# Tap weights in 64x64 quarters of the TensorE array, with regrouped products, in a two-layer convolution and local-attention kernel

## The chip, the cores and the metric

The kernel runs on one core of a Trainium2 chip, as one launch. The metric is the device time in microseconds. A core has five engines with a queue of instructions each: TensorE (PE), VectorE (DVE), ScalarE (ACT), GpSimd (POOL) and SyncE (SP, which here only starts DMAs). All data are float32.

## The reference, cut to what matters

Eight images of 256 channels and 64x64 pixels pass through two layers, each `x = x + layer(group_norm(x))`.

```python
# layer 0: an involution-like convolution, REL=32, OUT=256, SHARE=8, 3x3
x1, x2, x3 = conv1x1(x, w1), conv1x1(x, w2), conv1x1(x, w3)       # 32, 32, 256 channels
h = relu(bn(concat([x1, unfold3(reflect_pad(x2))])))              # 320 channels
h = relu(bn(conv1x1(h, cw1)))                                     # 32 channels: the inner map
w = conv1x1(h, cw2, cb2).reshape(B, 32, 9, H, W)                  # the tap weights
out = einsum("bgskhw,bgkhw->bgshw", unfold3(pad(x3)), w)          # 9 products, summed
# layer 1: local attention, 7x7, 4 heads, beside a dynamic depthwise convolution
att = softmax(q . (unfold7(k) + position)); out_att = att . unfold7(v)
wts = softmax(conv1x1(x, Wfc).reshape(B, 256, 9, H, W), axis=2)
out_conv = sum_k(depthwise3(relu(depthwise3(x, w1)), w2) * wts)   # depthwise kernels alike for all k
out = rate1 * out_att + rate2 * out_conv
```

What the change touches is layer 0: the inner map `h` of 32 channels, the tap weights `w` that one matrix per tap makes of it, and the products of each tap's weights with the shifted map `x3`.

## The kernel before, in words

**Blocks and steps.** A picture is cut into NB = 8 bands of R = 8 rows. The main loop runs over blocks `g`, one block being one band of one image in layer 1; layer 0 runs AHEAD = 12 blocks ahead of it, so that while layer 1 works at band `g`, layer 0 makes the bands `g + 10` to `g + 12`. For `g < 0` layer 0 is alone (the code says `alone`; here called the front). A block has STEPS = 8 steps `s`: two channel tiles `ct` of four steps `m` each.

**The order is written by hand.** The scheduler is off (`manual_schedule`): every engine runs its instructions in the order in which the program emits them. A step has six places, each ended by `advance()`; `after(n, f)` puts `f` off by `n` places. The functions `beside(g, s)` and `steer(g, s)` say what of layer 0, of the keys, queries and values, and of the loads is emitted in which step: lists `head`, `mid` and `end` are run at three places of a step.

**What a step does in layer 1.** In even steps TensorE makes the scores (`scores`, tile `sco`, 64x64 quarters of the array: two heads by two query tiles) for this step and the next. `masked` (VectorE) adds the mask and takes the maximum; `exponentials` (ScalarE, L772), a reciprocal of the sum `tot` (VectorE, L779) and `probabilities` (ScalarE, L781) make the softmax; one step later `transposed` (tile `ptp`, copied to `pt`) and `weighted_values` (tile `small`) use it, and `add_values` adds to the output `xr`. In each step two `branch_weights` (tile `pf`, L886) go through ScalarE's `ex` (L891), which POOL sums (L1106). The depthwise convolution is 32 taps of VectorE per block (`acc`, L843 and L869), taken from a list `todo`: two in the second place of a step, and in the fourth place two in even steps and the rest in odd ones. At a tile's end `depthwise_end` has ScalarE write `oc` (L879), two buffers; `dynamic_sum` has POOL make `tot` (L899, L902), VectorE its reciprocal `rec` (L907), and POOL multiply and add into `xr` (L908, L912, L913). `keys` makes `pk` on TensorE, which VectorE turns into `kb` (L714, L721): for the next block in step 7 and for the second channel tile in step 3, in the first and last band in step 6 and 2. `first_stats` takes group-norm statistics (L287) of a later image.

**What a block does in layer 0.** `small_maps` (x1 and x2; ScalarE writes them, L347 and L351) in steps 0 and 1; `value_maps` (x3: tile `p`, L375, written by ScalarE as `x3n`, L380) emitted at the end of step 0 and in step 1; `hidden_maps` with its parts `one` and `two` in steps 4 and 6 makes the inner map `h2n`. The band is held as four pieces of two rows: partition `32 q + c` holds channel `c` of piece `q`. `tap_weights` multiplies `h2n` (128 partitions, 2 x 66 columns) by `c2[:, k]`, a 128x128 matrix with four equal 32x32 blocks on its diagonal, into a PSUM tile `pw` (L470), and then emits the products (`prod`, L483: a sum of `pw` and bias times the shifted `x3q`, 8 channels of a group at once). POOL adds each product to `xg` (L491); in the front every third goes through TensorE instead (L504). After the last, `take` has VectorE take statistics (L519) and the band is stored (L529).

Two tuples set the order: `TAPS_AT` the steps at whose end each group of taps is multiplied, `PRODUCTS_AT` the places after which its products follow. In the front it is three groups of three taps; otherwise groups of 2, 2, 2, 2 and 1 at the ends of steps 1 to 5.

**Buffers.** PSUM tiles with the tag `gen` (`pf`, `ptp`, `pw`, `p`, `pk`, `pq`, `pv`) share four buffers: a tile takes the one that came free first in the program's order, and its first matmul waits for the last reader of the tile that was there. `sco` has one buffer, products two (tag `prod`), `ex` three.

Of the kernel before, what the change touches and what calls it, by code (L numbers as in the profile page):

```python
# [18 lines left out]
P = 128  # L19
C = 256  # L20
# [16 lines left out]
SHARE = C // REL  # L37
PIECE = SR * W
RUN = (SR - 1) * (W + 2) + W
TG = 2, 3  # L40
HP = W + 2
HR = R + 2

# [20 lines left out]
STEPS = NCT * NT // 2  # L64


TAPS_AT = (1, 2, 3, 4, 5), (0, 2, 4)
PRODUCTS_AT = ((1, 2),) * 5, ((7, 14, 10), (9, 17, 13), (12, 20, 16))


CB3, CBQ, CBK, CBP, CWP0, CWP1, CW1, CW2, CBV = 0, 1, 2, 3, 4, 5, 6, 15, 24
# [16 lines left out]
def conv_layers_kernel(ctx: ExitStack, tc: tile.TileContext, ins: dict, out: bass.AP):  # L88
# [33 lines left out]
    c1 = load("c1", [P, 3, REL])  # L122
    gq = load("gq", [P, P])
    gc = load("gc", [P, NCT, P])
    c2 = load("c2", [P, KK, P], now=False)
    wq = load("wq", [P, NCT, C], ins["wq"].rearrange("(t p) n -> p t n", p=P), now=False)
    wk = load("wk", [P, NCT, C], ins["wk"].rearrange("(t p) n -> p t n", p=P), now=False)
    wv = load("wv", [P, NCT, C], ins["wv"].rearrange("(t p) n -> p t n", p=P), now=False)
# [13 lines left out]
    for t in probs + x3n + h2n:  # L142
        nc.gpsimd.memset(t, 0.0)

    def inverse_root(v):
# [45 lines left out]
    def layer1_loads():  # L191


        last = w1.tile([P, NCT, 1, C], F32, tag="oc", name="last")
# [218 lines left out]
    def hidden_maps(b, i, alone):  # L413
# [26 lines left out]
        def relu(v):  # L440
            nc.scalar.activation(h2, v, AF.Relu, bias=bn2b, scale=bn2s)

        def one(home):
            ph = conv(home, 0, 2, 0, 1)
            after(1, lambda: hidden(2))
            after(2, lambda: nc.scalar.copy(h2, ph))

        def two(home):
            ph = conv(home, 2, 3, 2, 2)
            after(1, lambda: nc.vector.tensor_add(h2, ph, h2))  # L450
            after(3, lambda: relu(h2))

        hidden(0)
        after(3 if alone else 5, lambda: hidden(1))
        if alone:

            home = ps.tile([P, 4 * P], F32, tag="acc", name=f"ph_{b}_{i}")
            after(7, lambda: conv(home, 0, 2, 0, 2))
            after(8, lambda: hidden(2))
            after(12, lambda: after(4, lambda ph=conv(home, 2, 3, 0, 2): relu(ph)))  # L460
        return [two, one]

    def tap_weights(b, i, u, alone, at):


        im = images[b]
        first, n = TG[alone] * u, min(TG[alone], KK - TG[alone] * u)
        pw = ps.tile([P, n, SR * HP], F32, tag="gen", name=f"pw_{b}_{i}_{u}", bufs=4)
        for j in range(n):
            nc.tensor.matmul(  # L470
                pw[:, j], c2[:, first + j], h2n[i % 2].rearrange("p r c -> p (r c)"), start=True, stop=True
            )

        def product(j):
            k = first + j
            if alone and j == n - 1:
                prod = w1.tile([P, NCT, RP, W], F32, tag="yp", name=f"prod_{b}_{i}_{k}", bufs=3)
                prod = prod.rearrange("p t r c -> p (t r c)")[:, : SHARE * SR * HP]
                prod = prod.rearrange("p (s n) -> p s n", s=SHARE)
            else:  # L480
                prod = w0.tile([P, SHARE, SR * HP], F32, tag="prod", name=f"prod_{b}_{i}_{k}", bufs=2)
            at = k // 3 * HP + k % 3
            nc.vector.scalar_tensor_tensor(  # L483
                prod[:, :, :RUN], pw[:, j, :RUN].unsqueeze(1).to_broadcast([P, SHARE, RUN]),
                par[:, PCB2 + k : PCB2 + k + 1],
                im.x3q[i].rearrange("p s r c -> p s (r c)")[:, :, at : at + RUN], ALU.add, ALU.mult,
            )
# [24 lines left out]

        def take():
            x = im.xg[i]
            if i == 0:
                im.st1 = stat.tile([P, 2 * NB, 6], F32, tag="st1", name=f"st1_{b}")
            for t in range(2):
                v = x[:, t * SHARE // 2 : (t + 1) * SHARE // 2].rearrange("p s r c -> p (s r c)")
                nc.vector.bn_stats(im.st1[:, 2 * i + t, :], v)  # L519
            im.x1[i] = dram.tile([C, BAND], F32, tag="x1", name=f"x1_{b}_{i}")  # L520
            if alone:
                after(9, lambda: keep(nc.scalar))
            else:
                keep(nc.sync)

        def keep(queue):
            for q in range(NQR):
                v = im.xg[i][q * REL : (q + 1) * REL].rearrange("p s r c -> p s (r c)")
                queue.dma_start(out=pieces(im.x1[i], q), in_=v)  # L529

        for j in range(n):
            after(at[j], lambda j=j: product(j))
# [342 lines left out]

    def depthwise_end(b, i, ct, acc):

        oc = w1.tile([P, BAND], F32, tag="oc", name=f"oc_{b}_{i}_{ct}")
        nc.scalar.activation(oc, acc.rearrange("p r c -> p (r c)"), AF.Copy, scale=rate2)  # L879
        return oc  # L880

# [45 lines left out]
    def beside(g, s):  # L927
# [57 lines left out]
        if 0 <= g + AHEAD - 1 < B * NB and s == (2 if alone else 1):  # L985
            bh, ih = divmod(g + AHEAD - 1, NB)

            def hidden():
                parts = hidden_maps(bh, ih, alone)
                if not alone:  # L990
                    convs.extend(parts)

            end.append(hidden)
        if 0 <= g + AHEAD - 2 < B * NB and s in TAPS_AT[g < -1]:
            u = TAPS_AT[g < -1].index(s)
            end.append(
                lambda: tap_weights(*divmod(g + AHEAD - 2, NB), u, g < -1, PRODUCTS_AT[g < -1][u])
            )
        return head, mid, end

    def steer(g, s):
# [5 lines left out]
        if s == 2 and n % NB == 0 and 0 < n < B * NB:  # L1007
            scaled_weights(n // NB)
        if s == (3 if g < -1 else 7) and g + AHEAD0 < B * NB:
            first_stats(*divmod(g + AHEAD0, NB), n=40 if g < -1 else 9)  # L1010
        if s == 5 and 0 <= g + 1 < B * NB:
            bn, inx = divmod(g + 1, NB)
            xr = images[bn].xr[inx] = x_tile("xr", bn, inx)
# [10 lines left out]
    with tc.manual_schedule():  # L1024
# [21 lines left out]
        for g in range(-AHEAD, B * NB):  # L1046
            b, i = divmod(g, NB)
            for s in range(STEPS):
# [81 lines left out]
def _layout(inputs):  # L1130
# [29 lines left out]
    arr["par"] = par  # L1160

    c2 = a["a_cw2"].reshape(REL, KK, REL).transpose(2, 1, 0)
    arr["c2"] = np.zeros((P, KK, P), f)
    for q in range(NQR):
        arr["c2"][q * REL : (q + 1) * REL, :, q * REL : (q + 1) * REL] = c2

    chan = np.zeros((C, NCHAN), f)
    chan[:, CB3] = a["a_b3"]
# [43 lines left out]
```

## Time and profile before

| what | value |
|---|---|
| median of 3 runs | 3852.04 us (3850.59 to 3853.89) |
| the profiled execution's own time | 3854.63 us |
| its span, first to last instruction | 3852.8 us |
| mean granted TensorE clock | 0.994 |
| PE matmul busy | 3756.3 us, 97% |
| PE weight loads busy (beside the matmuls) | 2109.9 us, 55% |
| DVE busy | 3434.4 us, 89% |
| ACT busy | 2809.2 us, 73% |
| POOL busy | 3116.8 us, 81% |
| DMA, mean | 127 GB/s |

The profile lists instructions with the line of the program that made them, the tile written and those read (`prod<-pw,c_par,x3q`), and shapes as partitions x elements. A float32 matmul shows as two records of equal length; the 576 taps are 1152 records of `pw`. Records of TensorE overlap[...]: what an instruction costs TensorE's queue is the time from its start to the next one's start, not its length. In the timeline, equal instructions that follow each other are merged (`x4`), with the start of the first and the time to the end of the last; a bracket at the end gives the engine's idle time ahead of it and what ended that.

### The profile page before, as it was taken

The page shows a single profiled execution, that of the slowest core. Times are in us where ns is not written, and L with a number is a line of the kernel's source. Part 1 is how long each engine was busy: PE and PEld are TensorE (multiplying, and loading weights), DVE is VectorE, ACT ScalarE, POOL GpSimd, SP SyncE. Part 2 cuts the span into 40 slices and gives each one's busy share as a digit, 9 for nine tenths or more (in the row PEclk, how much of TensorE's full clock was granted, in tenths as well). Part 3 has the DMA queues.
Part 4 walks back from the last instruction along what each step waited for, and adds up shares of the span by engine and source line. Part 5 has one row for each costly group of instructions (what it writes and reads, how often), then busy time and mean ns, then how long its engine had stood idle before and what let it go on. Part 6 is the DMA issues. An engine that isn't in the chain of part 4 may idle for free.

```text
span 3852.8 us, 71646 instructions
## 1 busy us (share of the span) xinstructions
PE 3756.3 (97%) x24620; PEld 2109.9 (55%) x24620; DVE 3434.4 (89%) x7125; ACT 2809.2 (73%) x6770; POOL 3116.8 (81%) x2100
## 2 busy tenths in 40 slices
PE   6889999999999999999999999999999999999998
PEld 3445555555555555555555555555555555555554
DVE  6879999999999999899998999999999899978877
ACT  4457777777777777777777777777777777677776
POOL 4868888888897888888888888888888888855565
PEclk9999999999999999999999999999999999999999
DMA  8764544544444544544544544454544544232221
GB/s 247 210 177 128 142 118 129 151 126 118 133 135 131 145 123 115 148 135 127 136 116 142 142 125 120 126 149 125 136 115 117 138 119 114 74 97 78 79 67 37
DMA packets 438926, 490.14 MB, mean 127 GB/s; under 512 B 62016, under 2 KB 324256, under 8 KB 438304
## 3 DMA queue, kind: packets, MB, share of 16 engines
q1 hardware_dynamic: 421984, 469.79, 44.1%
q10 hardware_dynamic: 16576, 15.76, 1.3%
q8 instruction: 194, 3.18, 0.4%
q14 instruction: 172, 1.41, 0.1%
HBM read 343.76 MB, written 145.10 MB: 127 GB/s over the span
## 4 chain that ended last, share of the span: by engine, by line
PE 81%; POOL 10%; DVE 3%; DMA 2%; ACT 2%; issue 2%; SPq 1%; ACTq 0%; POOLq 0%; DVEq 0%
PE pf L886 39%; PE small L799 6%; PE ptp L787 6%; POOL xg L491 6%; PE pk L706 5%; PE pq L684 5%; PE sco L750 5%; PE p L375 5%; PE pv L601 5%; PE pw L470 2%; POOL ex L1106 2%; PE small L332 1%; DVE prod L483 1%; PE small L434 1%; DMA x<-x3n 1%
## 5 line engine op out<-in xcount | busy, mean ns | idle before, releaser
L886 PE MATMUL pf<-yp,c_wfc 128*128 128x512 f32 x4096 | 1916.8, 594 | 11.3 <-DVE prod L483 6.3
L491 POOL TENSOR_TENSOR xg<-xg,prod 128x1024 f32<-128x1024 f32 x549 | 1199.8, 2185 | 132.5 <-DVE prod L483 103.6
L886 PEld LDWEIGHTS pf<-yp,c_wfc 128*128 128x128 f32 x4096 | 739.6, 190 | 711.4 <-issue 654.7
L1106 POOL TENSOR_TENSOR ex<-ex,ex 128x1024 f32<-128x1024 f32 x384 | 908.8, 2367 | 68.5 <-ACT ex L891 65.0
L891 ACT ACTIVATE ex<-pf 128x512 f32<-128x512 f32 x1024 | 604.0, 590 | 347.9 <-PE pf L886 269.2
L843 DVE SCALAR_TENSOR_TENSOR acc<-yp,c_chan,acc 128x504 f32<-128x504 f32 (+3 forms) x1104 | 775.5, 702 | 63.2 <-ACT acc L834 42.8
L483 DVE SCALAR_TENSOR_TENSOR prod<-pw,c_par,x3q 128x1040 f32<-128x1040 f32 x576 | 732.7, 1294 | 107.9 <-PE pw L470 60.8
L869 DVE SCALAR_TENSOR_TENSOR acc<-hid,c_chan,acc 128x504 f32<-128x504 f32 (+3 forms) x1024 | 751.1, 733 | 18.1
L781 ACT ACTIVATE prob<-prob,tot 128x196 f32<-128x196 f32 x1024 | 412.9, 452 | 242.4 <-DVE tot L779 236.8
L772 ACT ACTIVATE prob<-prob,nmax 128x196 f32<-128x196 f32 x1024 | 458.2, 450 | 101.3 <-DVE nmax L764 101.2
L907 DVE RECIPROCAL rec<-tot 128x256 f32<-128x256 f32 x256 | 445.7, 1741 | 28.3 <-POOL tot L902 27.5
L789 ACT COPY pt<-ptp 112x512 f32<-112x512 f32 x511 | 295.9, 579 | 111.8 <-PE ptp L787 111.8
L764 DVE CUSTOM_DVE_ANT_0 prob<-sco,c_mask 128x196 f32<-128x196 f32 x1024 | 324.8, 355 | 31.0 <-PE sco L750 31.0
L787 PEld LDWEIGHTS ptp<-ident,prob 128*112 128x112 f32 x2044 | 227.3, 133 | 184.4 <-issue 132.7
L787 PE MATMUL ptp<-ident,prob 128*112 128x128 f32 x2044 | 319.5, 279 | 0.0
L908 POOL TENSOR_TENSOR tot<-tot,rec 128x256 f32<-128x256 f32 x254 | 185.8, 732 | 145.7 <-DVE rec L907 139.7
L799 PEld LDWEIGHTS small<-pt,vt 112*64 112x64 f32 x8144 | 258.6, 138 | 79.8 <-issue 60.5
L799 PE MATMUL small<-pt,vt 112*64 112x64 f32 x8144 | 294.2, 225 | 3.3 <-DMA vt<-vd 1.8
L601 PE MATMUL pv<-c_wv,yp 128*128 128x256 f32 x1056 | 253.5, 383 | 1.8 <-ACT yp L572 1.8
L902 POOL TENSOR_SCALAR tot<-tot 128x512 f32<-128x512 f32 x127 | 243.9, 1920 | 11.1
L470 PEld LDWEIGHTS pw<-h2n,c_c 128*128 128x128 f32 x1152 | 175.1, 191 | 139.9 <-issue 115.9
L375 PE MATMUL p<-xc,w3s 128*128 128x512 f32 x512 | 243.3, 598 | 0.0
(136 smaller groups left out, 4656.7 us busy)
## 6 DMA issues: line engine op xcount, KB each, us to landing
vt<-vd SPq DMA_DIRECT2D x512, 112.0 KB
x3q<-x SPq DMA_DIRECT2D x128, 264.0 KB
xc<-in_x SPq DMA_DIRECT2D x64, 512.0 KB
xg<-in_xg SPq DMA_DIRECT2D x64, 512.0 KB
yp<-x SPq DMA_DIRECT2D x128, 256.0 KB
xr<-x SPq DMA_DIRECT2D x64, 512.0 KB
out_x<-xr SPq DMA_DIRECT2D x64, 512.0 KB
xs<-in_x SPq DMA_DIRECT2D x57, 512.0 KB
```

The lines of the kernel that those rows point to most:

```text
L483: nc.vector.scalar_tensor_tensor(prod[:, :, :RUN], pw[:, j, :RUN].unsqueeze(1).to_broadcast([P, SHARE, RUN]), par[:, PCB2 + k : PCB2 + k + 1],
L491: nc.gpsimd.tensor_add(im.xg[i], im.xg[i], rows(prod))
L601: nc.tensor.matmul(pv[:, g], yp[:, kt, r : r + 2].rearrange("p r c -> p (r c)"), wv[:, kt], start=(kt == 0), stop=(kt == NCT - 1),)
L772: nc.scalar.activation(prob[:, h, :NKEY], prob[:, h, :NKEY], AF.Exp, bias=nmax[:, h : h + 1], scale=-1.0, accum_out=tot[:, h : h + 1],)
L787: nc.tensor.transpose(ptp[:, h, ch], prob[:, h, ch * CHUNK : (ch + 1) * CHUNK], ident)
L799: nc.tensor.matmul(po[half[h], :, t * TQ : (t + 1) * TQ], im.vt[i + ch, m][:n, t, (2 * ct + h) * HD : (2 * ct + h + 1) * HD], pt[:n, h, ch ...
L843: nc.vector.scalar_tensor_tensor(o, yp[:, ct, ra + dr : rb + dr, ca + dc : cb + dc], chan[:, ct, CW1 + k : CW1 + k + 1], o, ALU.mult, ALU.add,
L869: nc.vector.scalar_tensor_tensor(o, hid[:, ra + dr : rb + dr, ca + dc : cb + dc], chan[:, ct, CW2 + k : CW2 + k + 1], o, ALU.mult, ALU.add,)
L886: nc.tensor.matmul(pf, wfc[:, kt, 2 * m + j, ct * P : (ct + 1) * P], images[b].yp[i][:, kt, PAD : PAD + R], start=(kt == 0), stop=(kt == N ...
L891: nc.scalar.activation(ex[:, j].rearrange("p (r c) -> p r c", r=R), pf, AF.Exp)
L907: nc.vector.reciprocal(rec, v)
L1106: after(4, lambda ex=ex, exb=exb: nc.gpsimd.tensor_add(ex, ex, exb))
```

## The change

- `c2` becomes 128x64 per tap: each half of the partitions holds its own two 32x32 blocks. A tap is no longer one 128x128 matmul but two of 64x64 (two instructions each), which write the lower and the upper half of the PSUM tile.
- A second copy of the inner map, `h2s`, has its halves exchanged: ScalarE writes it with two activations of 64 partitions just ahead of the one that writes `h2n`. A row half of the array can so make both halves of a tap: one from `h2n`, one from `h2s`. One tap of a group runs in the lower rows, another in the upper ones, each into a tile of its own.
- Outside the front the taps form four groups, (0, 1 | 2), (3 | 4), (5 | 6), (7 | 8), at the ends of step 7 of the block before and of steps 1, 3 and 5, each just ahead of scores. In the front the groups stay, all in the lower rows, two quarters at a time.
- The products of the first group follow after 1, 2 and 3 places, of the others after 1 and 2. Products have three buffers instead of two.
- In even steps one depthwise tap instead of two is emitted in the fourth place; the odd step that follows takes it.
- `first_stats` takes its statistics after 15 places instead of 9 (outside the front); the last front block's inner map is written 4 places later.
- `oc` has one buffer instead of two, which makes room.

In the program as built, TensorE has two small matmuls for each of the 576 large ones, ScalarE 128 activations more, POOL one memset more; VectorE has as many instructions as before in another order; SP's queue is the same.

```diff
+HALF = P // 2
-TAPS_AT = (1, 2, 3, 4, 5), (0, 2, 4)
-PRODUCTS_AT = ((1, 2),) * 5, ((7, 14, 10), (9, 17, 13), (12, 20, 16))
+TAPS = (((0, 1), (2,)), ((3,), (4,)), ((5,), (6,)), ((7,), (8,))), tuple(((k, k + 1, k + 2), ()) for k in (0, 3, 6))
+TAPS_AT = (-1, 1, 3, 5), (0, 2, 4)
+PRODUCTS_AT = ((1, 2, 3), (1, 2), (1, 2), (1, 2)), ((7, 14, 10), (9, 17, 13), (12, 20, 16))
...
-    c2 = load("c2", [P, KK, P], now=False)
+    c2 = load("c2", [P, KK, HALF], now=False)
...
+    h2s = const.tile([P, SR, HP], F32, name="h2s")
...
         def relu(v):
+            for a, z in ((0, HALF), (HALF, 0)):
+                o, z = slice(a, a + HALF), slice(z, z + HALF)
+                nc.scalar.activation(h2s[o, :, :W], v[z], AF.Relu, bias=bn2b[z], scale=bn2s[z])
             nc.scalar.activation(h2, v, AF.Relu, bias=bn2b, scale=bn2s)
...
-            after(12, lambda: after(4, lambda ph=conv(home, 2, 3, 0, 2): relu(ph)))
+            after(12, lambda: after(gap, lambda ph=conv(home, 2, 3, 0, 2): relu(ph)))
...
-        first, n = TG[alone] * u, min(TG[alone], KK - TG[alone] * u)
-        pw = ps.tile([P, n, SR * HP], F32, tag="gen", name=f"pw_{b}_{i}_{u}", bufs=4)
-        for j in range(n):
-            nc.tensor.matmul(
-                pw[:, j], c2[:, first + j], h2n[i % 2].rearrange("p r c -> p (r c)"), start=True, stop=True
-            )
+        lots = TAPS[alone][u]
+        ks = [k for lot in lots for k in lot]
+        n = len(ks)
+        pws = [
+            ps.tile([P, len(lot), SR * HP], F32, tag="gen", name=f"pw_{b}_{i}_{u}_{r}", bufs=4)
+            for r, lot in enumerate(lots) if lot
+        ]
+        side = [slice(0, HALF), slice(HALF, P)]
+        for m in range(len(lots[0])):
+            for q in range(2):
+                for r, lot in enumerate(lots):
+                    if m < len(lot):
+                        h2 = (h2n[i % 2] if q == r else h2s)[side[r]].rearrange("p r c -> p (r c)")
+                        nc.tensor.matmul(pws[r][side[q], m], c2[side[r], lot[m]], h2, start=True, stop=True)
+        weights = [pw[:, m] for pw, lot in zip(pws, lots) for m in range(len(lot))]
...
-                prod = w0.tile([P, SHARE, SR * HP], F32, tag="prod", name=f"prod_{b}_{i}_{k}", bufs=2)
+                prod = w0.tile([P, SHARE, SR * HP], F32, tag="prod", name=f"prod_{b}_{i}_{k}", bufs=3)
...
-        oc = w1.tile([P, BAND], F32, tag="oc", name=f"oc_{b}_{i}_{ct}")
+        oc = w1.tile([P, BAND], F32, tag="oc", name=f"oc_{b}_{i}_{ct}", bufs=1)
...
-            first_stats(*divmod(g + AHEAD0, NB), n=40 if g < -1 else 9)
+            first_stats(*divmod(g + AHEAD0, NB), n=40 if g < -1 else 15)
...
-                    for _ in range(2 if m % 2 == 0 else len(todo)):
+                    for _ in range(1 if m % 2 == 0 else len(todo)):
                         todo.pop(0)()
```

More of the change, by code (lines that the diff above doesn't have):

```diff
@@ L39 @@
 RUN = (SR - 1) * (W + 2) + W
-TG = 2, 3
+HALF = P // 2
 HP = W + 2
@@ L141, in conv_layers_kernel @@
     h2n = [const.tile([P, SR, HP], F32, name=f"h2n_{i}") for i in range(2)]
-    for t in probs + x3n + h2n:
+    h2s = const.tile([P, SR, HP], F32, name="h2s")
+    for t in probs + x3n + h2n + [h2s]:
         nc.gpsimd.memset(t, 0.0)
@@ L191, in layer1_loads @@
     def layer1_loads():
-        last = w1.tile([P, NCT, 1, C], F32, tag="oc", name="last")
+        last = w1.tile([P, NCT, 1, C], F32, tag="oc", name="last", bufs=1)
         for f in late:
@@ L411, in x_by_group, with hidden_maps @@
         nc.sync.dma_start(out=t.rearrange("p s r c -> p (s r c)"), in_=ins["xg"][b, i])
-    def hidden_maps(b, i, alone):
+    def hidden_maps(b, i, alone, gap):
         im = images[b]
@@ L466, in tap_weights @@
         im = images[b]
-        first, n = TG[alone] * u, min(TG[alone], KK - TG[alone] * u)
-        pw = ps.tile([P, n, SR * HP], F32, tag="gen", name=f"pw_{b}_{i}_{u}", bufs=4)
-        for j in range(n):
-            nc.tensor.matmul(
-                pw[:, j], c2[:, first + j], h2n[i % 2].rearrange("p r c -> p (r c)"), start=True, stop=True
-            )
+        lots = TAPS[alone][u]
[13 more added lines that the diff above has]
+        weights = [pw[:, m] for pw, lot in zip(pws, lots) for m in range(len(lot))]
         def product(j):
-            k = first + j
+            k = ks[j]
             if alone and j == n - 1:
@@ L480, in product @@
             else:
-                prod = w0.tile([P, SHARE, SR * HP], F32, tag="prod", name=f"prod_{b}_{i}_{k}", bufs=2)
+                prod = w0.tile([P, SHARE, SR * HP], F32, tag="prod", name=f"prod_{b}_{i}_{k}", bufs=3)
             at = k // 3 * HP + k % 3
             nc.vector.scalar_tensor_tensor(
-                prod[:, :, :RUN], pw[:, j, :RUN].unsqueeze(1).to_broadcast([P, SHARE, RUN]),
+                prod[:, :, :RUN], weights[j][:, :RUN].unsqueeze(1).to_broadcast([P, SHARE, RUN]),
                 par[:, PCB2 + k : PCB2 + k + 1],
@@ L988, in hidden @@
             def hidden():
-                parts = hidden_maps(bh, ih, alone)
+                parts = hidden_maps(bh, ih, alone, 4 if g < -1 else 8)
                 if not alone:
@@ L993, in beside @@
             end.append(hidden)
[L994 to L998, printed above, removed]
+        for gt, st in ((g, s), (g + 1, s - STEPS)):
+            front = gt < -1
+            if 0 <= gt + AHEAD - 2 < B * NB and st in TAPS_AT[front]:
+                u = TAPS_AT[front].index(st)
+                end.append(
+                    lambda gt=gt, u=u, front=front: tap_weights(
+                        *divmod(gt + AHEAD - 2, NB), u, front, PRODUCTS_AT[front][u]
+                    )
+                )
         return head, mid, end
@@ L1162, in _layout @@
     c2 = a["a_cw2"].reshape(REL, KK, REL).transpose(2, 1, 0)
-    arr["c2"] = np.zeros((P, KK, P), f)
+    arr["c2"] = np.zeros((P, KK, HALF), f)
     for q in range(NQR):
-        arr["c2"][q * REL : (q + 1) * REL, :, q * REL : (q + 1) * REL] = c2
+        o = q * REL % HALF
+        arr["c2"][q * REL : (q + 1) * REL, :, o : o + REL] = c2
     chan = np.zeros((C, NCHAN), f)
```

## The prediction

> **What bounds the kernel now.** I read the page first, then five long windows of equal length, then one regular block (image 4, band 1, from 2146.70 us, with the end of the block before it) engine by engine in the timeline.
>
> ```profile
> PE 3756.3 (97%) x24620; PEld 2109.9 (55%) x24620; DVE 3434.4 (89%) x7125; ACT 2809.2 (73%) x6770; POOL 3116.8 (81%) x2100
> ```
> ```profile
> 2050.00:2500.00 450.00, 447.61 (x2980) 253.12 (x2979) 415.13 (x868) 338.28 (x820) 388.59 (x257) 1.00 0.48 132
> ```
>
> The columns of the second line are the window, its length, then busy time of PE, weight loads, DVE, ACT and POOL. TensorE is busy 99.5% of the stretch, VectorE 92%. So in the long middle part TensorE sets the pace and any instruction taken from its queue counts, as long as the other queues keep up; VectorE has 8% to spare and no more. A regular block is 56.9 us from its first scores to the next block's.
>
> The tap weights in TensorE's timeline:
>
> ```profile
> 2102.35 0.61 PE L470 MATMUL pw<-h2n,c_c 128*128 128x132 f32 x4
> 2102.90 0.92 PE L750 MATMUL sco<-kb,qb 64*64 64x196 f32 x16
> 2103.74 1.15 PE L799 MATMUL small<-pt,vt 112*64 112x64 f32 x32
> ...
> 2126.35 0.61 PE L470 MATMUL pw<-h2n,c_c 128*128 128x132 f32 x4
> 2126.80 1.88 PE L886 MATMUL pf<-yp,c_wfc 128*128 128x512 f32 x4
> ```
>
> From start to start, four instructions (two taps) take 0.45 ahead of pf and 0.55 ahead of scores: 0.22 a tap, and 0.10 for going over to the 64x64 tiles. Nine taps are 1.98 us of each block.
>
> The stretch from the keys of step 7 to the second value map, in the same block's TensorE, VectorE and ScalarE timelines:
>
> ```profile
> 2141.02 1.88 PE L706 MATMUL pk<-yp,c_wk 128*128 128x512 f32 x4
> ...
> 2146.70 0.92 PE L750 MATMUL sco<-kb,qb 64*64 64x196 f32 x16
> ...
> 2157.29 1.02 PE L375 MATMUL p<-xc,w3s 128*128 128x512 f32 x2
> ```
> ```profile
> 2143.47 1.28 DVE L519 BATCH_NORM_STATS2 st<-xg 128x6 f32<-128x512 f32 x2
> 2144.67 0.74 DVE L714 SCALAR_TENSOR_TENSOR kb<-pk,c_chan,pe 128x512 f32<-128x512 f32 x1
> 2145.32 0.53 DVE L721 SCALAR_TENSOR_TENSOR kb<-pk,c_chan,pe 128x16 f32<-128x16 f32 x3
> 2145.76 1.53 DVE L869 SCALAR_TENSOR_TENSOR acc<-hid,c_chan,acc 128x504 f32<-128x504 f32 x2
> 2147.20 0.16 DVE L779 RECIPROCAL tot<-tot 128x2 f32<-128x2 f32 x1
> ```
> ```profile
> 2152.46 0.80 ACT L781 ACTIVATE prob<-prob,tot 128x196 f32<-128x196 f32 x2
> 2153.16 1.40 ACT L347 ACTIVATE x<-small,bias 32x252 f32<-32x252 f32 x3
> 2154.57 0.47 ACT L351 ACTIVATE x<-small,bias 32x256 f32<-32x256 f32 x1
> 2155.06 0.60 ACT L891 ACTIVATE ex<-pf 128x512 f32<-128x512 f32 x1
> ```
>
> What to see: ScalarE runs these without a gap, and its ex ends at 2155.66, 1.63 us before the p at 2157.29. In the built program, before and after, that p waits for this ex, whose PSUM buffer it takes. Pk ends at 2142.90, but VectorE comes to kb only at 2144.67: it is 1.8 us late, and so never waits for pk. Both margins matter below.
>
> [...] sixteen score instructions, 196 columns each, take 0.85 us, where 196 columns of a full-width matmul are 0.164 (pf: 1.72 for 4x512), 2.6 us one after the other; and the change costs the 0.10 above.[...]
>
> **The change part by part, in a regular block.**
> *TensorE.* The scores make four rounds of four tiles in 0.75 (0.85 less 0.10 on leaving the mode), 0.187 a round against 0.164 of streaming. A round of 132 columns streams 0.111; with 0.01 to 0.025 on top, 0.12 to 0.135. One pair of taps is two rounds, 0.25; the group of three taps is four, 0.5. Sum 0.5 + 3 x 0.25 = 1.25 against 1.98: **0.73 saved**. All four groups stand ahead of scores, so the change of mode moves to the front of the group and is not added. Over 55 blocks this is 40 us, if nothing waits.
> *VectorE.* As many instructions as before, reordered. Products stood two at the turn into each of steps 2 to 5 and one at 6; now three stand at the turn into step 0 and two at each of 2, 4, 6. One conv tap per pair of steps goes from even to odd, first_stats (1.20) into step 1. This evens the load, and VectorE comes to step 6 without lag: from the turn into step 2 it has four products (4.9 us) less before it than now, where it takes up the last product at 2136.19, 3.0 us after its weights. It therefore comes early to kb in step 7 and must now **wait for pk**. Behind kb stand, in the program's order, up to the recip that releases ScalarE's prob: kb 1.09, two taps 1.44, BN stats 1.20, recip 0.12, three taps 2.17, product 1.22, masks 0.57, xr 0.52, product 1.22, two taps 1.44, product 1.22, recip 0.16. With 0.04 to start (a product began 0.04 after its pw ended) this is 12.4 us after pk. ScalarE then needs 0.04 + prob 0.70 + maps 1.90 + ex 0.60 = 3.2, and p 0.05 more: p can start **15.7 us after pk ends**. TensorE would be there after 14.39 (2157.29 - 2142.90) + 0.5 for the new group = 14.9. So p waits 0.8. The 1.63 of margin is used up, because prob starts 8.15 after the scores of step 0 where it started 5.76 after them.
> *Sum of a regular block:* -1.98 + 1.25 + 0.8 = +0.1. On top, p's weight load is no longer hidden (0 to 0.19), and the next ptp waits for x3n, which runs 5.9 after that ex where TensorE needs 5.7 (0 to 0.2). I take +0.2, with 0 to +0.5 as ends. The regular blocks with value maps ahead are bands 1 to 6: 39 of them, **+8 us**.
> *Band 7:* its keys are made in step 6, so VectorE does not wait in step 7; the recip is 1.3 earlier and the margin holds: 7 x -0.73 = -5. *Band 0:* keys in step 6 too, but the one-row depthwise piece puts a ScalarE round trip ahead of the products: between -0.73 and +0.3, I take 7 x -0.4 = -3. The last two blocks with taps have no value maps: -1.5.
> *ScalarE* gets 128 halves of the relu; a full one is 0.46 to 0.48 and the same columns are worked, so 0.4 each, 0.8 a block at step 6, where it stands idle about 1 us at a time (prob for tot, 1.04). Cost nothing; without that cover 0.8 a block.
> *POOL* does the same work (85% busy), xg adds filling its wait of 3.5 us for the x maps. Adds in step 2 need the buffer of the product three back, long done. *One oc buffer:* ScalarE's oc in step 4 must wait for POOL's xr; adding the adds of 2.2 and the other POOL rows, xr ends 14.8 after the scores of step 2 and oc comes at 15.7. Nothing, with 0.9 to spare. SP's queue keeps its order.
> *Front (first 250 us).* One row half only, two tiles at a time, so no tap gets faster; a change of mode each side, 0.1 to 0.2 per group, two groups of a block on its chain, eight blocks: +2 to +3. The third product buffer takes away up to the 6 us that products wait for POOL there, though the chain runs mostly through TensorE, ScalarE and DMA. I take +1, from -5 to +6. The smaller c_c2 load and h2s's memset: nothing, hidden by the input loads. The waits with 0 given could also gain: bound 0.1 a block.
>
> *All:* +8 - 5 - 3 - 1.5 + 1 = about 0. The profiled execution took 3854.6 us (span 3852.8), 2.6 above the median 3852.0; the sum stands against its own time, and moved to the median gives **3852**.
>
> **Rivals.**
> 1. *The gain stays.* VectorE, or the ScalarE queue, is faster than my chain and p does not wait: 3852 - 40 = 3812; with half of it, 3832. For it: TensorE at 99.5%. Against: every link of the 15.7 is a measured row.
> 2. *Slower: the oc buffer.* If POOL comes over 0.9 us later than worked out, ScalarE stands at oc at the turn of steps 3 and 4, with the acc of the next conv, pt and ex behind it, and VectorE's taps wait in turn. 0.6 a block beyond the point over 39 blocks: +23, 3875.
> 3. *The quarters don't overlap* in these small shapes: 36 instructions of 0.111 are 4.0 us instead of 1.98, +2 a block, 3960. The scores speak against it.
>
> **How the numbers follow.** The wait taking the gain back: 0.61, its own range 3838 to 3872 (regular blocks 0 to +0.5, band 0 and front to their ends). The gain stays: 0.20. The oc buffer or another second wait: 0.14. No overlap: 0.05. A measurement tells about 0.2%, 8 us, from no change; of the first case 0.13 lies faster, 0.32 within and 0.16 slower. Faster 0.33, same 0.32, slower 0.35. The range 3828 to 3882 leaves out the lower part of rival 1 and rival 3.
>
> **What would show it.** Right: pw groups of 0.25 and 0.5; VectorE idle at kb behind pk once a regular block; p waiting for ex by some 0.8, about 40 times, and blocks of 57.0 us. Band 7 shorter by 0.7. Wrong: no wait at p and blocks of 56.2; oc waiting for xr; or pw groups of 0.4 and more.

## The result and the profile after

The changed kernel took **3898.2 us** (median of 4 runs, 3893.4 to 3901.1), the kernel before 3851.7 beside it: ratio **1.0117**, 95% interval 1.0101 to 1.0133, so it is slower by about 46 us. The forecast was 3852, with 3828 to 3882 as range. The profiled execution took 3901.1 us, its span 3899.3.

The first part of the page after, and the window that was shown of before:

```profile
PE 3739.2 (96%) x25772; PEld 2038.1 (52%) x25772; DVE 3399.9 (87%) x7125; ACT 2868.5 (74%) x6898; POOL 3120.7 (80%) x2101
```
```profile
2050.00:2500.00 450.00, 436.44 (x3021) 238.16 (x3020) 401.53 (x848) 343.00 (x826) 378.83 (x256) 1.00 0.46 127
```

TensorE has 17 us less busy time in all and works 97% of the stretch where it was 99.5%: it stands still 13.6 us of 450, against 2.4. VectorE and POOL are less busy there than before, ScalarE by 4.7 us more, 76% in all. So no engine became the bound by its load; waits did.

What TensorE waits for, over the whole span (waited for: us in total, times, longest):

```profile
PE p L377 <- ACT ex L905: 43.9, 52, 1.8
PE ph L436 <- ACT hid L426: 22.1, 12, 4.0
PE small L813 <- ACT x L353: 21.3, 52, 0.4
PE pg_a L244 <- DVE mv_a L238: 20.8, 1, 20.8
PE pf L900 <- DVE prod L497: 10.0, 6, 1.7
```

The first and the third are new, with 65 us (small had waited once, 1.5 us); ph and pg_a lie in the front and were there before. The tap weights themselves, at the turn into image 4, band 2, and what follows them:

```profile
2237.75 0.32 PE L485 MATMUL pw<-h2n,c_c 64*64 64x132 f32 x1
...
2238.25 0.86 PE L764 MATMUL sco<-kb,qb 64*64 64x196 f32 x14
2239.04 1.15 PE L813 MATMUL small<-pt,vt 112*64 112x64 f32 x32
...
2249.59 1.98 PE L377 MATMUL p<-xc,w3s 128*128 128x512 f32 x4 [0.65 <-ACT ex L905]
...
2254.78 1.15 PE L813 MATMUL small<-pt,vt 112*64 112x64 f32 x32 [0.41 <-ACT x L353]
```

From the first pw to small it is 1.29; scores alone took 0.85, so three taps cost 0.44. The same for every place of this block, from start to start in us, in the kernel before, in the one after, and in the fastest kernel of the experiments (experiment 8, "final" here); places that did not change are left out:

| TensorE, image 4, band 2 | before | after | final |
|---|---|---|---|
| (taps and) scores of step 0 | 0.85 | 1.29 | 1.29 |
| ptp to the second p | 0.44 | 1.25 | 0.44 |
| that p | 1.72 | 1.82 | 1.72 |
| pf, (change of mode,) taps and scores of step 2 | 3.11 | 3.36 | 2.88 |
| pf and taps of step 3 | 2.17 | 1.72 | 1.72 |
| pf, taps and scores of step 4 | 3.12 | 2.89 | 2.89 |
| two pf and taps of step 5 | 3.88 | 3.43 | 3.43 |
| pf, taps and scores of step 6 | 2.89 | 2.88 | 2.89 |
| sum against before | | +0.5 | -0.9 |

VectorE and ScalarE between the keys of step 7 and those two waits, same block:

```profile
2233.99 0.75 DVE L728 SCALAR_TENSOR_TENSOR kb<-pk,c_chan,pe 128x512 f32<-128x512 f32 x1 [0.94 <-PE pk L720]
...
2239.99 1.30 DVE L497 SCALAR_TENSOR_TENSOR prod<-pw,c_par,x3q 128x1040 f32<-128x1040 f32 x1
...
2244.93 1.29 DVE L497 SCALAR_TENSOR_TENSOR prod<-pw,c_par,x3q 128x1040 f32<-128x1040 f32 x1
2246.14 0.15 DVE L793 RECIPROCAL tot<-tot 128x2 f32<-128x2 f32 x1
```
```profile
2246.33 0.81 ACT L795 ACTIVATE prob<-prob,tot 128x196 f32<-128x196 f32 x2 [2.28 <-DVE tot L793]
2247.05 1.40 ACT L349 ACTIVATE x<-small,bias 32x252 f32<-32x252 f32 x3
2248.45 0.47 ACT L353 ACTIVATE x<-small,bias 32x256 f32<-32x256 f32 x1
2248.95 0.60 ACT L905 ACTIVATE ex<-pf 128x512 f32<-128x512 f32 x1
2249.57 0.69 ACT L382 ACTIVATE x3n<-p,bias 128x512 f32<-128x512 f32 x1
...
2251.98 0.81 ACT L795 ACTIVATE prob<-prob,tot 128x196 f32<-128x196 f32 x2
2252.80 1.43 ACT L349 ACTIVATE x<-small,bias 32x252 f32<-32x252 f32 x3
2254.26 0.47 ACT L353 ACTIVATE x<-small,bias 32x256 f32<-32x256 f32 x1
```

VectorE stands at kb until pk ends (2233.95), and from there to the end of the reciprocal (2246.29) it does not pause: 12.3 us. ScalarE then works from prob at 2246.33 to the second half of the maps at 2254.73 without a pause either. Two waits hang on this one queue: ex releases p at 2249.59, and the maps' second half releases small at 2254.78, since `small` has one PSUM buffer and x1 and x2 lie in it. Ahead of that, ScalarE had stood 2.28 us at step 0's prob; in the old order it did not stand there at all (image 4, bands 1 to 7).

Not every band lost the same. From first scores to first scores, before and after (median of the same band over images 1 to 4), and the change summed over all images (4 and 5 together):

| band | 0 | 1 | 2 | 3 | 4, 5 | 6 | 7 |
|---|---|---|---|---|---|---|---|
| before | 58.1 | 56.9 | 56.9 | 59.6 | 56.9 | 56.5 | 60.8 |
| after | 59.8 | 57.7 | 57.3 | 60.4 | 57.3 | 56.7 | 63.9 |
| sum | +8.6 | +5.6 | +3.4 | +5.3 | +4.6 | +0.2 | +14.8 |

With +4.2 before the first scores these make the 46 us. Band 7 stands out. Its step 6 (image 3) in TensorE's timeline, and the granted clock there:

```profile
2102.71 0.62 PE L801 MATMUL ptp<-ident,prob 128*112 128x128 f32 x4
2105.00 3.65 PE L900 MATMUL pf<-yp,c_wfc 128*128 128x512 f32 x4 [1.67 <-DVE prod L497]
2108.47 2.55 PE L720 MATMUL pk<-yp,c_wk 128*128 128x512 f32 x8
```
```profile
2104.00:2105.00 1.00, 0.00 (x1) 0.03 (x1) 1.00 (x3) 0.84 (x4) 0.83 (x2) 1.00 1.14 190
2105.00:2107.00 2.00, 2.00 (x3) 0.97 (x4) 1.96 (x5) 0.00 (x0) 2.00 (x1) 0.52 1.13 202
2107.00:2109.00 2.00, 2.00 (x4) 0.73 (x4) 1.21 (x1) 0.25 (x1) 2.00 (x2) 0.63 1.09 329
2109.00:2112.00 3.00, 3.00 (x11) 1.71 (x10) 1.59 (x7) 2.51 (x6) 2.84 (x4) 1.00 0.82 227
```

(Window, length, busy time and instructions of PE, weight loads, DVE, ACT, POOL, then the granted clock.) The pf waits for the PSUM buffer that the product of tap 8 reads last. It starts 2.29 after ptp instead of the usual 0.49: 1.8 us late, where it was 1.2 late before. Then a pf that usually takes 1.72 takes 3.47, at a granted clock of 0.52 from 2105 to 2107. That happened in four of the six such places of this execution; at 1.7 us each it is some 7 of band 7's 14.8.

### The profile page after: what moved, and what is told of

Same layout as the page of the kernel before. It is cut to its first block, busy times and chain, and to the rows that moved or that the text cites. A ratio compares the mean times of both kernels' runs of the same rounds, so it can differ in the third digit from the quotient of the medians.

```text
span 3899.3 us, 73816 instructions
## 1 busy us (share of the span) xinstructions
PE 3739.2 (96%) x25772; PEld 2038.1 (52%) x25772; DVE 3399.9 (87%) x7125; ACT 2868.5 (74%) x6898; POOL 3120.7 (80%) x2101
## 4 chain that ended last, share of the span: by engine, by line
PE 70%; DVE 12%; ACT 8%; POOL 4%; issue 3%; DMA 2%; SPq 1%; ACTq 0%; POOLq 0%; DVEq 0%
PE pf L900 35%; PE small L813 6%; PE ptp L801 5%; PE pv L615 5%; PE pq L698 5%; PE pk L720 5%; DVE prod L497 4%; PE sco L764 3%; ACT x L349 2%; POOL xg L505 2%; PE p L377 2%; DVE acc L883 2%; PE pw L485 2%; DVE acc L857 2%; ACT prob L786 1%
## 5 line engine op out<-in xcount | busy, mean ns | idle before, releaser
L900 PEld LDWEIGHTS pf<-yp,c_wfc 128*128 128x128 f32 x4096 | 747.5, 191 | 741.4 <-issue 653.5
L857 DVE SCALAR_TENSOR_TENSOR acc<-yp,c_chan,acc 128x504 f32<-128x504 f32 (+3 forms) x1104 | 773.7, 701 | 55.9 <-ACT acc L848 35.5
L813 PEld LDWEIGHTS small<-pt,vt 112*64 112x64 f32 x8144 | 258.3, 138 | 104.7 <-issue 60.2
L377 PE MATMUL p<-xc,w3s 128*128 128x512 f32 x512 | 249.0, 610 | 43.9 <-ACT ex L905 43.9
L793 DVE RECIPROCAL tot<-tot 128x2 f32<-128x2 f32 x512 | 81.6, 159 | 198.4 <-ACT prob L786 197.4
```

The source lines that it names most:

```text
L813: nc.tensor.matmul(po[half[h], :, t * TQ : (t + 1) * TQ], im.vt[i + ch, m][:n, t, (2 * ct + h) * HD : (2 * ct + h + 1) * HD], pt[:n, h, ch ...
L857: nc.vector.scalar_tensor_tensor(o, yp[:, ct, ra + dr : rb + dr, ca + dc : cb + dc], chan[:, ct, CW1 + k : CW1 + k + 1], o, ALU.mult, ALU.add,
L900: nc.tensor.matmul(pf, wfc[:, kt, 2 * m + j, ct * P : (ct + 1) * P], images[b].yp[i][:, kt, PAD : PAD + R], start=(kt == 0), stop=(kt == N ...
```

## The experiments

**Theory:** the order of VectorE's queue. Three products stand between VectorE's restart at kb and step 0's reciprocal; ScalarE's queue, and p and small behind it, come too late. **Rival A:** the quarters themselves or the two half activations cost the time. **Rival B:** the single oc buffer.

**1. One product behind the reciprocal.**

```diff
-PRODUCTS_AT = ((1, 2, 3), (1, 2), (1, 2), (1, 2)), ((7, 14, 10), (9, 17, 13), (12, 20, 16))
+PRODUCTS_AT = ((1, 2, 4), (1, 2), (1, 2), (1, 2)), ((7, 14, 10), (9, 17, 13), (12, 20, 16))
```

> The changed kernel with the third product of the first group one place later, behind the reciprocal of step 0 instead of ahead of it. Theory (VectorE's order: three products ahead of step 0's reciprocal make ScalarE's prob, maps and ex late, TensorE then waits at p and, in step 2, at small): the chain from pk to p loses one product, 1.22 us, so the waits at p (0.8 in a regular block, 1.6 in band 0) and at small (0.4) go; regular block 57.3 to 56.1, total 3898 - 52 x 1.2 = about 3834, below the kernel before. Rival A (the quarters or the extra half activations themselves cost the time): within 5 us of 3898. Rival B (the one oc buffer): within 5 us of 3898.

Measured 3836.0, ratio to before 0.9954 (0.9937 to 0.9970). One number in one tuple turns 46 us lost into 18 gained. Regular blocks went from 57.3 to 56.1. TensorE's waits:

```profile
PE pf L900 <- DVE prod L497: 9.9, 6, 1.7
PE small L813 <- ACT x L353: 7.4, 18, 0.4
...
PE p L377 <- ACT ex L905: 3.1, 7, 0.5
```

Both new waits shrink together, 65 us to 10.5, though nothing near p or small was touched; quarters, half activations and oc buffer are those of the changed kernel. This settles for the theory, and against A and B as the main cause. In regular blocks about 0.2 stayed ahead of small, too short for the list of waits but plain from start to start (scores to small 1.00 in place of 0.80). The six waits at pf in band 7 are untouched, and the clock fell in four of them here too.

**2. The conv taps back.**

```diff
-                    for _ in range(1 if m % 2 == 0 else len(todo)):
+                    for _ in range(2 if m % 2 == 0 else len(todo)):
```

> The changed kernel with the conv taps back where they were: two in the second half of an even step instead of one. Theory: in step 7 the three taps between kb and the reciprocal become two, 0.72 us off the chain from pk to p, and step 6 gets 0.72 more, which VectorE's wait at kb (1.2 us on average) takes up: p waits 0.1 instead of 0.8 in a regular block and small hardly, about -1.0 a block, total about 3850. Rivals A (quarters) and B (oc buffer): no change, 3898; if the even load matters more, slower than 3898.

Measured 3865.0, 1.0029 (1.0021 to 1.0036): a gain of 33 us where 48 was expected. The p of a regular block starts 15.0 us after pk instead of 15.65, and the waits of p fall from 43.9 to 21.9 us in total. So the tap counts on the chain to p, as worked out. Small did not follow: 21.5 us in 52 waits, as in the changed kernel. The lines above say why. ScalarE's second maps end 5.2 us after the ex that releases p (2254.73 against 2249.55), and TensorE, once p has started, comes to small in 4.7 (p 1.82 and the 2.88 of the final column). As long as p starts right behind ex, small is late by the same amount, however late ex is.

**3. The diagonal quarters, in the changed order.**

```diff
-            for a, z in ((0, HALF), (HALF, 0)):
-                o, z = slice(a, a + HALF), slice(z, z + HALF)
-                nc.scalar.activation(h2s[o, :, :W], v[z], AF.Relu, bias=bn2b[z], scale=bn2s[z])
...
-                        h2 = (h2n[i % 2] if q == r else h2s)[side[r]].rearrange("p r c -> p (r c)")
-                        nc.tensor.matmul(pws[r][side[q], m], c2[side[r], lot[m]], h2, start=True, stop=True)
+                        h2 = h2n[i % 2][side[q]].rearrange("p r c -> p (r c)")
+                        nc.tensor.matmul(pws[r][side[q], m], c2[side[q], lot[m]], h2, start=True, stop=True)
```

> The changed kernel in its own order, but each tap from the two diagonal quarters of its own half of the map, one tap at a time, and no exchanged copy: TensorE needs as long per tap as before, ScalarE is rid of the half activations. Theory: TensorE gets 0.9 a block more, of which the first group's 0.44 lies ahead of the late p and only shortens its wait: +0.4 to +0.5 a block, about 3898 + 25 = 3922, so that the order by itself costs 70 us against the kernel before. Rival A (the half activations on ScalarE cost the time): 3870 or less.

Measured 3904.5, 1.0130 (1.0115 to 1.0145); expected about 3922. The p still starts 15.65 us after pk, to the hundredth: the half activations, absent here, have no part in that chain. Regular blocks went from 57.3 to 57.8, inside what was expected (0.4 to 0.5), as p and small wait less (29.8 and 10.5 us in all) when TensorE comes later. The rest of the miss is band 7, 1.9 shorter in most images: there the wait is for VectorE anyway, and after the slightly shorter idle the clock fell once in six places. With p late, 0.9 a block more of TensorE's work cost some 5 us in all: in a regular block half of it went where TensorE would have waited, in bands 0 and 1 more (0.2 is left), and band 7 came out shorter.

**4. Quarters at the old places.**

The kernel before with the quarters, the exchanged copy and half-width c2, and five groups of two taps, the last of one; outside the front all else is as it was (cut to the order):

```diff
+TAPS = (((0,), (1,)), ((2,), (3,)), ((4,), (5,)), ((6,), (7,)), ((8,), ())), tuple(((k, k + 1, k + 2), ()) for k in (0, 3, 6))
 TAPS_AT = (1, 2, 3, 4, 5), (0, 2, 4)
 PRODUCTS_AT = ((1, 2),) * 5, ((7, 14, 10), (9, 17, 13), (12, 20, 16))
```

> The kernel before with quarters alone: five groups of two taps (the last of one) at its own places, products at its own places, two product buffers, two oc buffers, conv taps and statistics where they were; the two half activations are there. Theory: two groups ahead of scores save 0.22 each (0.45 to 0.226), two ahead of pf and pk save 0.22 each less two changes of mode of 0.10, the single one nothing: -0.45 a block over 55 blocks, 3852 - 25 = about 3827, no wait at p. Rival A (quarters or the half activations cost the time): 3870 or more. A smaller effect of the half activations would show as 3840 to 3852.

Measured 3862.9 (median of 19 runs; a twentieth took 11170 us, for a reason that is not known, and is left out), 1.0018 (1.0011 to 1.0025): slightly slower than before, where 25 us of gain were expected. A miss, and not for the reason of rival A: p has its old margin of 1.63 and starts 14.39 after pk. Two things eat the gain. A group between pf and pk changes the mode twice (first fence below: from the first pw to pk 0.39, and the pf ahead takes 1.81 for 1.72, the pk after 1.82 for 1.72), so two taps there cost 0.58 against 0.45: +0.13 each where I had put 0. And a pair now takes two of the four gen buffers, one for each tap. In band 0 TensorE then waits three times for ScalarE to read such a buffer, 0.32 at the pair's second tile and 0.31 and 0.84 at two later pf (second fence, image 4), where it had waited 0.24 before. Regular blocks gain 0.2, band 0 loses 1.4. Whether the second tile is needed is open. In experiment 3 the twelve instructions of taps 0, 1 and 2 start in six pairs, by the edit one of each row half, 0.013 us apart, a pair every 0.11 us (0.16 after the first). Two of these taps share a tile, so in at least two pairs both row halves write one tile at once, each its own partitions, without delay. Both halves on the same partitions of one tile were not tried.

```profile
2229.73 0.32 PE L485 MATMUL pw<-h2n,c_c 64*64 64x132 f32 x1
...
2230.12 1.98 PE L720 MATMUL pk<-yp,c_wk 128*128 128x512 f32 x4
```
```profile
2114.20 0.44 PE L485 MATMUL pw<-h2n,c_c 64*64 64x132 f32 x2
2114.96 0.33 PE L485 MATMUL pw<-h2s,c_c 64*64 64x132 f32 x2 [0.32 <-ACT ex L905]
...
2131.48 1.98 PE L900 MATMUL pf<-yp,c_wfc 128*128 128x512 f32 x4 [0.84 <-ACT vc L622]
```

So the quarters gain little at the old places. They pay ahead of scores; it is the products that may not come along.

**5. Two products behind the reciprocal.**

```diff
-PRODUCTS_AT = ((1, 2, 3), (1, 2), (1, 2), (1, 2)), ((7, 14, 10), (9, 17, 13), (12, 20, 16))
+PRODUCTS_AT = ((1, 4, 5), (1, 2), (1, 2), (1, 2)), ((7, 14, 10), (9, 17, 13), (12, 20, 16))
```

> The changed kernel with two of the first group's three products behind step 0's reciprocal. With one of them behind it, p still waited 3 us in all and small 7 us, both at image turns, and regular blocks had 0.44 to spare at p. Theory (a margin that is used up, not a price per product): the second product brings only what was left, regular blocks stay at 56.1, band 0 loses up to 1.0: 3836 - 10 = about 3826. Rival (each product ahead of the reciprocal costs its 1.22 us): another 52 x 1.2, about 3774. If the late products make POOL's additions or a PSUM buffer late: above 3836.

Measured 3802.6, 0.9878 (0.9863 to 0.9893). Neither number was met: some 30 us below experiment 1 by the ratios, where 10 were expected and 62 by the rival. Regular blocks are 55.9 for 56.1 (the last 0.2 at small), band 0 57.5 for 58.6, band 3 58.1 for 59.2, band 6 54.5 for 55.1, and in this execution the clock did not fall in band 7 (four falls of 1.7 us in the one compared). So the price is that of a margin used up, and not of each product, but small had not got its margin back with one product. One caution: with this order p takes the buffer that the product frees instead of ex's, so it has no wait for ex left to measure; experiment 1 is the cleaner one for that wait.

**6. The last pair ahead of the masks.**

```diff
-PRODUCTS_AT = ((1, 2, 3), (1, 2), (1, 2), (1, 2)), ((7, 14, 10), (9, 17, 13), (12, 20, 16))
+PRODUCTS_AT = ((1, 2, 4), (1, 2), (1, 2), (1, 1)), ((7, 14, 10), (9, 17, 13), (12, 20, 16))
```

> Third product behind the reciprocal as before, and besides both products of the last group ahead of the masks of step 6, where the second stood behind them. In band 7 TensorE waits 1.85 us at pf of step 6 for that second product, whose PSUM buffer pf takes, and in four of six such places its clock then was at half for some 3.4 us (1.7 us lost). Theory: the product comes 1.0 us earlier, the wait is 0.85, the clock stays; band 7 shorter by 1.0 to 2.7, about 6 x 2.1 = 13: about 3823, other bands as they were. Rival (the later masks make prob of step 6 late in every block): 3836 or more.

Measured 3816.5, 0.9902 (0.9886 to 0.9919): 20 us below experiment 1 by the ratios; expected 13. Band 7 fell from 63.0 to 60.2, and no pf ran at half clock. TensorE's waits at pf:

```profile
PE pf L900 <- DVE prod L497: 2.9, 6, 0.5
```

9.9 us in six waits became 2.9. The other gains were not foreseen here: small's 0.2 in the regular blocks, 1.0 in each band 3 and 0.7 in band 6, just as in experiment 5. Why this edit brings them too was not followed up.

**7. The delay without the quarters.** The kernel before, with four statistics instructions (result unused) in step 0:

```diff
+                if g >= 0 and s == 0:
+                    for _ in range(4):
+                        nc.vector.bn_stats(spent, wfc[:, 0, :2].rearrange("p k c -> p (k c)"))
                 if g >= 0:
                     probabilities(prob, tot)
```

> The kernel before, with four statistics instructions of 0.6 us whose result nobody reads put into VectorE's queue ahead of step 0's reciprocal: 2.4 us more ahead of it, as much as the change moved there; no quarters. Theory: p's margin of 1.63 becomes a wait of 0.8, p's weight load shows with 0.1, small of step 2 waits up to 0.4: +0.9 to +1.3 a block over 52 blocks, 3854 + 47 to 68, about 3910. Rival A (the quarters or the half activations cost the time): at most +10, 3864.

And the same lines behind `probabilities`:

> The kernel before with the same four statistics instructions directly behind step 0's reciprocal. It is as much more work for VectorE (92% to 96% busy), but prob, the maps and ex of ScalarE are not behind it. Theory (place, not load): 3854 to 3866. Rival (VectorE's load itself): as much as with the four ahead of the reciprocal, 3900 or more.

Measured 3944.7 ahead, 1.0243 (1.0228 to 1.0258), and 3904.6 behind, 1.0133 (1.0118 to 1.0149). Both are above what the theory expected. Their difference, 40 us or 0.77 in each of 52 blocks, is the price of the place alone: p waits 30.6 us in all with the four ahead (first fence) and not at all with them behind. The other 53 us are the rival's: 2.8 us more of VectorE in step 0 (177.5 us over 64 blocks) make it late in steps 2 and 3 as well. The second kernel's waits (second fence) show where: in most regular blocks at pf of step 3 and at small of step 2.

```profile
PE p L376 <- ACT ex L892: 30.6, 52, 1.6
```
```profile
PE pf L887 <- ACT ex L892: 17.5, 33, 1.7
PE small L800 <- ACT x L352: 13.2, 37, 1.5
```

So the prediction's "8% to spare" on VectorE was no cushion in the steps where it would be needed, and the place accounts for 40 of these 93 us. In the changed kernel VectorE's work was only moved, not added.

**8. Both places, and the value of the quarters.** Two products behind the reciprocal and the last pair ahead of the masks, `((1, 4, 5), (1, 2), (1, 2), (1, 1))`:

> The changed kernel with two products of the first group behind step 0's reciprocal, and both products of the last group ahead of the masks of step 6. Theory: the two places add up; against the kernel with two behind alone (3803) only band 7's wait at pf of step 6 changes, 1.85 to about 0.7, six times: 3803 - 7 = about 3796, p and small without waits. Rival (with VectorE's masks of step 6 later, something else of step 6 or 7 comes late now that TensorE is faster): 3803 or more.

Measured **3791.9**, 0.9840 (0.9825 to 0.9855): 62 us faster than the kernel before and 106 faster than the changed one. Theory had about 3796: the two places add up. The same window, and the places in TensorE's and ScalarE's timelines that were shown of after:

```profile
2050.00:2500.00 450.00, 449.12 (x3201) 248.18 (x3200) 420.03 (x882) 356.13 (x860) 393.82 (x263) 1.00 0.48 133
```
```profile
2181.44 0.60 PE L801 MATMUL ptp<-ident,prob 128*112 128x128 f32 x4
2181.88 1.88 PE L377 MATMUL p<-xc,w3s 128*128 128x512 f32 x4
```
```profile
2177.04 0.80 ACT L795 ACTIVATE prob<-prob,tot 128x196 f32<-128x196 f32 x2
```

TensorE is busy 99.8% of the stretch; ptp to p is 0.44 with no bracket; prob starts 5.9 after the scores at 2171.13, where it was 8.3 in the changed kernel and 5.8 before.

The diagonal quarters of experiment 3 with two products behind the reciprocal:

> Two products of the first group behind the reciprocal, as in the kernel of 3803, but each tap from the two diagonal quarters of its own half, one tap at a time, without the exchanged copy: TensorE's time per tap is that of the kernel before. Theory (with no wait at p, TensorE's 0.9 a block counts in full): 3803 + 0.9 x 55 = about 3850, level with the kernel before. Rival (the new order by itself was worth something): 3840 or less. Rival (another engine bounds by now, the quarters bring little): under 3825.

Measured 3841.6, 0.9963 (0.9949 to 0.9977); its pair with the exchanged copy, experiment 5, has 0.9878. So with p and small no longer late the quarters are worth 0.85% of 3852, some 33 us, and 0.9 in a regular block (56.8 to 55.9). The 12 us that the diagonal kernel itself gains on the one before are more than the theory's 4, and lie between it and the first rival: regular blocks are level (56.8 and 56.9), while bands 0, 3 and 6 are 4, 4 and 7 us shorter in all. They come with the new order; which part of it was not tried.

And experiment 8 with the conv taps two and two:

> As the kernel with two products behind and the last pair ahead of the masks, with the conv taps two and two as they were before. Theory: in the changed kernel the moved tap cost 0.6 a block because it lay ahead of the late reciprocal; with that margin back it costs nothing, so putting it back changes nothing: within 6 us of that kernel (about 3796). Rival (the moved taps cost by themselves): 3775 or less. If the even load is needed: 3805 or more.

Measured 3794.6, 0.9843 (0.9829 to 0.9858): the same as with the taps moved. Worth 33 us in experiment 2, the tap is worth nothing once two of the products stand behind the reciprocal.

## Why the prediction was wrong, point by point

The forecast was no change, the result +46 us. Of the miss some 20 lie in band 7, 12 in band 0, 12 in bands 1 to 6 and 3 in the front. The first wait, at p, was forecast rightly for a regular block; what failed is the step from there to what else waits, and to the other kinds of block.

- **TensorE's saving:** right in kind, under-sized. Worked out as 0.73 a block; the table's places without waits give 0.9 (final column). A pair of taps ahead of scores cost 0.23 and three taps 0.44, where I had 0.25 and 0.5, so the quarters do overlap and rival 3 is out. No change of mode was added, as said.
- **The chain from pk to p:** right. VectorE waits at kb (70.8 us in 58 waits); 12.3 us to the reciprocal for 12.4 worked out; p starts 15.65 after pk for 15.7, and waits 0.81 for 0.8. So rival 1 is out too. Its weight load shows with 0.10, inside the bound of 0 to 0.19.
- **"The next ptp waits for x3n":** put at 0 to 0.2, this step failed in every block with value maps. I followed ScalarE's queue from the late ex to the x3n that ends 5.9 after it, and asked only for the reader of that x3n. Just ahead of it in the queue stands the second half of the maps, and small, which it releases, comes on TensorE ahead of that ptp. Small waited 0.41 in each of 52 blocks, 21 us, and the ptp behind it not at all. A late queue has to be followed, instruction by instruction, until it meets an idle gap of its engine; small's wait ends 8.4 us after the late prob, the next gap of ScalarE comes after 14.
- **Regular blocks:** +0.2 taken, 0 to +0.5 as ends. Measured +0.5 in most (from start to start -0.9, p 0.81, its weight load 0.10, small 0.48), 19 us for bands 1 to 6, the last blocks included, against 8 - 1.5 worked out.
- **Band 7:** -5 worked out, +14.8 measured; the largest error. "VectorE does not wait in step 7; the recip is 1.3 earlier and the margin holds" has a false second half. VectorE did not wait there, because it came from step 6 with two products and the conv taps and no gap at all from 2050 on; its recip came 8.3 after the scores, later than in a regular block (8.1), and p waited 1.0. And I had not looked at band 7's own step 6, where pf already waited for a product before: with two products at that turn instead of one it waited 0.6 more, and in four of six places the clock fell behind that idle time.
- **Band 0:** -3 worked out, +8.6 measured. The upper bound I gave, +0.3 a block, was too low: p waits 1.8 there (image 4), as VectorE stands 3.4 us at the one-row piece's ScalarE round trip ahead of all three products, and small waits besides.
- **Half activations, POOL, the oc buffer:** no run contradicts the costs of nothing. The time from pk to p is the same with and without the half activations (experiment 3). ScalarE's oc waits for VectorE's acc (86.7 us in 96 waits, 1.1 at most) and not for POOL's xr; rival 2 did not happen, and the final kernel has one oc buffer too.
- **Front:** +1 worked out, +4.2 measured, within the ends; yet first scores lay between 231 and 246 us in kernels with that same front, so no more can be said.
- **The range** ended at 3882. It held the p wait's uncertainty in regular blocks, but took bands 7 and 0 as small gains with margins that I had inferred and not read. The rival on the slower side had the right form, a second wait on ScalarE's queue, at the wrong instruction.
- **The order of ScalarE's queue,** on which the chain rests: in the kernel before, at the start of image 4, band 1, ScalarE stood 1.61 us at prob, which started at 2147.39, and the ex behind it started at 2148.11. The pf of that ex had ended at 2146.77 (2144.89 and 1.88), so the order of the queue shows in the last 0.6 of the 1.61 alone.

## What to carry to other kernels

When work is moved into a stretch, read which short instruction behind it releases another engine, and put the movable work behind that instruction: here a kernel with three products ahead of a 0.15 us reciprocal was 46 us slower than before, and with two of them behind it 49 us faster. If a queue becomes late by some amount, follow it instruction by instruction to its next idle gap and ask of each one who waits for it. Repeat that for every kind of block, since the irregular ones (here bands 0 and 7) have their own last wait. When a first wait shrinks and a second does not, see whether the second starts from the end of the first.

## What was unexpected of the hardware

**Behind 1.66 to 1.67 us of idle time TensorE's clock stood at half in some places and not in others.** In band 7's step 6 (image 3 of the changed kernel), behind an idle time of 1.67 us, the granted clock was 0.50 from 2105.5 to 2108.0, and pf's instructions took 0.853 instead of 0.429 for some 3.4 us, which costs 1.7. In another image, behind 1.66 us, it was 1.00 for the whole pf (1636.3 to 1638.3). In the profiles, half clock came in 4 of 6 such places in the changed kernel, 4 of 6 in experiment 1, 1 of 6 in experiment 2, 0 of 6 in experiment 5, all with 1.64 to 1.67 idle. With about 1.5 idle (the two diagonal kernels) it was 1 of 6 each, with 1.1 or less (before, experiments 6 and 8) none. The length of the idle time alone does not decide it: p of band 0 starts behind the same 1.64 to 1.66 of idle time in the changed kernel and in experiment 2, twelve times together, and the clock fell behind none of them. Ahead of band 7's pf TensorE had run 2.5 us of small tiles and a ptp before it stood still, ahead of p full-width pf and a ptp; whether that decides it was not tried. Six falls of 1.7 are 10 us at most; how much of the spread of the runs they make is open, since the first scores alone lay up to 15 us apart.
